# Turning attention's weights by way of DRAM and VectorE instead of TensorE

## The chip, the cores and the metric

The kernel runs on one core of a Trainium2 chip. A core has a matrix engine (TensorE, PE in the profile; its weight loads are PEld), VectorE (DVE), ScalarE (ACT), GpSimd (POOL) and SyncE (SP), an on-chip memory of 128 partitions, a matmul result memory (PSUM) of 8 banks of 128 x 512 f32, and 16 DMA engines to DRAM. The metric is the time of one execution in device microseconds. All data are f32.

## The reference

The input is two images of 128 channels by 64 x 64 pixels. Layer 0 is a group norm, a neighbourhood attention of 7 x 7 and two small feed-forward steps. Layer 1 takes each image as 4096 tokens of 128 numbers. Its attention is plain, with q for queries, keys and values alike, and each token barred from itself:

```python
def _L1_attn_ref(q):                      # q: (2, 4096, 128), layer-normed tokens
    scale = 1.0 / np.sqrt(128)
    sim = jnp.einsum('blh,bmh->blm', q, q) * scale
    sim = jnp.where(jnp.eye(4096, dtype=bool)[None], -1e9, sim)
    attn = jax.nn.softmax(sim, axis=-1)
    return jnp.einsum('blm,bmh->blh', attn, q)

t = t + _L1_attn_ref(_ln_t(t))
t = t + _L1_ffn_ref(_ln_t(t), sigma, phi, M_u, M_phi_plus, M_phi_minus, log_weights, gumbel)
```

The second part (`_L1_ffn_ref`) is a long convolution with 16 filters, summed through 32 matrices of 128 x 128, with three short lags, in one of four branches that the weights pick. The diff does not touch what is computed.

## The kernel before

The program has three stages. Layer 0 runs first (to about 345 us), in an order written out by hand. Then layer 1's attention runs for image 0 and image 1 (345 to 1256 us). Last comes the convolution (to the end), written by hand for TensorE. The attention stage stands outside such a hand-made order: the framework places the instructions on the engines' queues, and in the trace TensorE's order within a pair is that of the source. On its queue an engine runs its instructions in order.

**Attention by pairs of chunks.** The 4096 tokens are 8 chunks of 512. Because q serves as query and key, the scores are symmetric, and each pair (a, c) of chunks with a <= c is computed once: 36 pairs an image, 8 of them on the diagonal. For a pair, the helper `weights(a, c, k)` is called for k = 0 to 3. Each call makes one score product of 128 tokens of chunk a by 512 tokens of chunk c (line 918, into a PSUM tile `bank`), and ScalarE takes the exponential into a tile `e` and sums its rows into `part` (line 926). The scores of the next pair are made while the present pair's are used.

A weight block has two uses. As it lies, with chunk a's tokens on the partitions, it is the right operand of the products that add to chunk c's output (PSUM tile `other`, line 983). For chunk a's output it must be turned, so that chunk c's tokens lie on the partitions. `turned(a, c, m, es)` does that: four TensorE transposes of 128 x 128 into a `bank` (line 942), and one VectorE operation that copies them to the tile `et` and sums the rows (line 945). Then `onto` multiplies `et` and adds to chunk a's output (PSUM tile `own`, line 956). These products wait in the list `late` and follow within two steps. A pair off the diagonal thus has 4 score products, 4 `other` products, 16 transposes and 4 `own` products. At the end of a pair VectorE adds `other` to the result `xa` (lines 995 and 997), and when a chunk's last product is in, it adds `own` (lines 960 and 962). `other` and `own` have one PSUM buffer each, `bank` has six.

On the diagonal, only the upper blocks are computed; `weights` turns the earlier ones by TensorE (line 932), and one VectorE operation copies and sums them (line 933). Line 924 adds a large negative number to the diagonal of the scores.

**Fill work.** After each of a pair's four steps `fill()` takes one piece from a list of other work: what is left of layer 0 (`drain`), the filters' transforms (`filters`, GpSimd's additions at line 1246), the tokens of image 1 (`tokens`), the layer norm and transform of each finished chunk (`after`, lines 1010 to 1071, with GpSimd's power at line 173 between VectorE's operations), the short lags (`short_lags`, line 1101), and the mixing of 32 matrices from loaded tiles `st` (`mixed`, lines 1171 to 1176). The transformed tokens are stored to DRAM by SP (`us`, lines 1043 and 1048).

GpSimd issues four DMAs in all (line 795, loads of image 1 at the start). ScalarE's queue issues a few near the start (lines 300 to 304). All other DMAs are on SP's queue.

Of the kernel before, what the change touches and what calls it, by code (L numbers as in the profile page):

```python
# [8 lines left out]
F32 = mybir.dt.float32  # L9
# [14 lines left out]
MASKED = -1.0e30  # L24

# [76 lines left out]
def kernel(  # L102
# [767 lines left out]
    with ap_:  # L870
        tp = ap_.enter_context(tc.tile_pool(name="l1_t", bufs=1, side="right"))
        ep = ap_.enter_context(tc.tile_pool(name="l1_e", bufs=8, side="right"))
        sp = ap_.enter_context(tc.tile_pool(name="l1_s", bufs=2, side="right"))
        ps_o = ap_.enter_context(tc.tile_pool(name="l1_ps_o", bufs=1, space=PSUM))
        ps_m = ap_.enter_context(tc.tile_pool(name="l1_ps_m", bufs=6, space=PSUM))
# [13 lines left out]
        one = tp.tile([P, 512], F32, name="one")  # L889
        nc.gpsimd.memset(one, 1.0)  # L890
# [6 lines left out]
        def attention(b, fill):  # L897
# [12 lines left out]
            pairs = [(a, c) for a in range(8) for c in range(a, 8)]  # L910
            chunk = lambda a: slice(CHUNKS[a] * 512, (CHUNKS[a] + 1) * 512)

            def weights(a, c, k, left=()):
# [3 lines left out]
                ps = bank()  # L917
                nc.tensor.matmul(  # L918
                    ps[:, lo:], lhsT=cm[b][:, n * P : (n + 1) * P],
                    rhs=cm[b][:, CHUNKS[c] * 512 + lo : (CHUNKS[c] + 1) * 512], start=True, stop=True,  # L920
# [4 lines left out]
                e = ep.tile([P, 512], F32, tag="e", name="e")  # L925
# [3 lines left out]
                if lo:  # L929
                    pt = bank()  # L930
                    for j in range(k):
                        nc.tensor.transpose(pt[:, j * P : (j + 1) * P], left[j][:, lo : lo + P], ident)
                    nc.vector.tensor_tensor_reduce(
                        e[:, 0:lo], pt[:, 0:lo], one[:, 0:lo], 1.0, 0.0, ALU.mult, ALU.add, part[:, n, 8:9]
                    )
                return e

            def turned(a, c, m, es):

                pt = bank()  # L940
                for k in range(4):
                    nc.tensor.transpose(pt[:, k * P : (k + 1) * P], es[k][:, m * P : (m + 1) * P], ident)  # L942
                et = ep.tile([P, 512], F32, tag="et", name="et", bufs=4)
                n = 4 * CHUNKS[c] + m
                nc.vector.tensor_tensor_reduce(  # L945
                    et, pt, one, 1.0, 0.0, ALU.mult, ALU.add, part[:, n, a : a + 1]
                )
                return et

            own = None  # L950

            def onto(a, n, e, first, last):
                nonlocal own
                if first:
                    own = ps_o.tile([P, 512], F32, tag="own", name="own")
                nc.tensor.matmul(own, lhsT=tok[b][:, n, :], rhs=e, start=first, stop=last)  # L956
                if last:
                    xs = xa[b][:, chunk(a)]
                    if a:
# [762 lines left out]
```

## Time and profile before

| What | Value |
|---|---|
| Median of 3 runs | 2070.3 us (2065.34 to 2070.57) |
| The profiled execution: its own time | 2070.71 us |
| The profiled execution: span from first to last instruction | 2068.7 us |
| Mean granted TensorE clock | 0.989 |
| `turned`'s transposes, line 942 | 896, of 273 ns (median) each, overlapping |
| Their evictions, line 945 | 224, of 686 ns (median) each |
| `own` products from `et`, line 956 | 448 passes, two a product |
| `other` products, line 983 | 448 passes, two a product |
| Largest group of the run, line 1436 (convolution) | 206.2 us of VectorE |

The profile is of one execution. It gives every instruction its engine, source line, start and duration. "Idle before" is the time that an engine stood still before a group of instructions, with the instruction that ended the wait. Matmuls overlap: a row's mean duration is longer than the distance between two of them, so the cost of one in a row is read from the distance of the starts. Every f32 product of 512 columns is recorded as two passes. "GB/s" and "DMA share" are what the 16 DMA engines moved and how busy they were. The chain is the line of work that ended last, followed back from the end.

### The profile page before, as it was taken

The page shows a single profiled execution, that of the slowest core. Times are in us where ns is not written, and L with a number is a line of the kernel's source. Part 1 is how long each engine was busy: PE and PEld are TensorE (multiplying, and loading weights), DVE is VectorE, ACT ScalarE, POOL GpSimd, SP SyncE. Part 2 cuts the span into 40 slices and gives each one's busy share as a digit, 9 for nine tenths or more (in the row PEclk, how much of TensorE's full clock was granted, in tenths as well). Part 3 has the DMA queues.
Part 4 walks back from the last instruction along what each step waited for, and adds up shares of the span by engine and source line. Part 5 has one row for each costly group of instructions (what it writes and reads, how often), then busy time and mean ns, then how long its engine had stood idle before and what let it go on. Part 6 is the DMA issues. An engine that isn't in the chain of part 4 may idle for free.

```text
span 2068.7 us, 52809 instructions
## 1 busy us (share of the span) xinstructions
PE 1997.5 (97%) x21368; PEld 1436.1 (69%) x21368; DVE 997.7 (48%) x3458; ACT 733.5 (35%) x1974; POOL 472.9 (23%) x781
## 2 busy tenths in 40 slices
PE   6899998999999999999999999999999999999998
PEld 4677775554555554554455554799999899999987
DVE  5899996444544445335733446333333333333332
ACT  3789885322322323212222322222222222222222
POOL 4466887215000000000000000022222121222211
PEclk8999999999999999999999999999999999999999
DMA  4222223003000001004200002222222123222211
GB/s 152 62 61 62 61 60 53 13 21 107 2 25 26 26 26 52 26 0 117 83 26 26 26 26 77 76 67 67 67 67 61 47 58 101 66 67 67 67 45 42
DMA packets 239506, 112.82 MB, mean 55 GB/s; under 512 B 118287, under 2 KB 237215, under 8 KB 238752
## 3 DMA queue, kind: packets, MB, share of 16 engines
q1 hardware_dynamic: 238338, 105.95, 18.9%
q8 instruction: 169, 2.77, 0.6%
q0 software_dynamic: 576, 2.10, 0.3%
q10 hardware_dynamic: 350, 1.41, 0.2%
q14 instruction: 73, 0.60, 0.1%
HBM read 74.78 MB, written 34.63 MB: 53 GB/s over the span
## 4 chain that ended last, share of the span: by engine, by line
PE 80%; DVE 7%; DMA 4%; POOL 4%; ACT 2%; SPq 2%; issue 1%; DVEq 0%; POOLq 0%; ACTq 0%
PE acc L1450 27%; PE own L956 11%; PE bank L918 9%; PE other L983 8%; PE pc L1431 7%; PE bank L942 4%; PE bank L343 2%; PE bank L201 1%; PE bank L1058 1%; PE bank L553 1%; DMA st<-in_m_minus_dram 1%; DMA st<-in_m_plus_dram 1%; ACT p L540 1%; PE bank L1101 1%; PE pc L1489 1%
## 5 line engine op out<-in xcount | busy, mean ns | idle before, releaser
L1436 DVE COPY y<-pc 128x512 f32<-128x512 f32 x320 | 206.2, 686 | 351.4 <-PE pc L1431 351.2
L926 ACT ACTIVATE e<-bank 128x512 f32<-128x512 f32 (+3 forms) x288 | 161.6, 561 | 519.6 <-PE bank L918 396.5
L1450 PE MATMUL acc<-y,mpl 32*128 32x256 f32 x5120 | 324.4, 380 | 0.8 <-DVE af L1460 0.8
L1450 PE MATMUL acc<-y,mmi 32*128 32x256 f32 x5120 | 316.7, 375 | 0.0
L1436 ACT COPY y<-pc 128x512 f32<-128x512 f32 x320 | 171.9, 589 | 400.9 <-PE pc L1431 396.1
L1450 PEld LDWEIGHTS acc<-y,mpl 32*128 32x128 f32 x5120 | 290.0, 186 | 8.2 <-DVE af L1460 1.8
L1450 PEld LDWEIGHTS acc<-y,mmi 32*128 32x128 f32 x5120 | 291.4, 185 | 3.8
L918 PE MATMUL bank<-cm 128*128 128x512 f32 (+3 forms) x576 | 277.4, 564 | 1.4 <-DVE y L664 1.4
L956 PE MATMUL own<-et,tok 128*128 128x512 f32 x448 | 230.2, 600 | 8.4 <-DVE part L945 8.1
L983 PE MATMUL other<-e,tok 128*128 128x512 f32 x448 | 229.9, 595 | 4.9 <-DVE xa L995 4.9
L1431 PE MATMUL pc<-ct,ut 32*128 32x256 f32 x2560 | 215.6, 382 | 5.6 <-DMA ut<-us 3.7
L945 DVE CUSTOM_DVE_ANT_0 et<-bank,one 128x512 f32<-128x512 f32 x224 | 146.1, 687 | 128.6 <-PE bank L942 128.4
L1461 POOL TENSOR_TENSOR af<-af 128x512 f32<-128x512 f32 x39 | 49.7, 1275 | 593.8 <-DVE af L1460 528.1
L173 POOL TENSOR_TENSOR ln_rs<-ln_rs,mhalf 128x4 f32<-128x4 f32 x24 | 24.2, 1009 | 703.6 <-DVE ln_rs L172 703.5
L1431 PEld LDWEIGHTS pc<-ct,ut 32*128 32x128 f32 x2560 | 175.7, 189 | 12.0 <-DMA ut<-us 4.5
L956 PEld LDWEIGHTS own<-et,tok 128*128 128x128 f32 x448 | 82.9, 190 | 121.8 <-issue 60.8
L983 PEld LDWEIGHTS other<-e,tok 128*128 128x128 f32 x448 | 81.7, 190 | 95.0 <-issue 86.9
L942 PEld LDWEIGHTS bank<-ident,e 128*128 128x128 f32 x896 | 103.0, 141 | 46.1 <-issue 39.4
L918 PEld LDWEIGHTS bank<-cm 128*128 128x128 f32 x576 | 94.5, 191 | 54.2 <-issue 38.9
L540 ACT ACTIVATE p<-p,mn 128x196 f32<-128x196 f32 x256 | 114.4, 449 | 13.7 <-DVE mn L530 13.0
L942 PE MATMUL bank<-ident,e 128*128 128x128 f32 x896 | 117.1, 274 | 0.0
L1039 DVE TENSOR_TENSOR ub<-bank,uo 128x256 f32<-128x256 f32 (+1 forms) x192 | 59.5, 373 | 71.1 <-ACT uo L1036 70.2
(258 smaller groups left out, 2530.8 us busy)
## 6 DMA issues: line engine op xcount, KB each, us to landing
ut<-us SPq DMA_DIRECT2D x160, 128.0 KB
us<-ub SPq DMA_DIRECT2D x128, 128.0 KB
ct<-gs SPq DMA_DIRECT2D x320, 40.0 KB
vw<-vd SPq DMA_DIRECT2D x256, 49.0 KB
ct<-gs SPq DMA_DIRECT2D x320, 32.0 KB
vd<-v SPq DMA_DIRECT2D x128, 32.0 KB
st<-in_m_plus_dram SPq DMA_DIRECT2D x16, 256.0 KB
us<-ub SPq DMA_DIRECT2D x128, 32.0 KB
```

The costliest lines, as they stand in the source:

```text
L540: nc.scalar.activation(p, p, AF.Exp, bias=t[name + "mn"][:, h : h + 1], scale=-1.0, accum_out=t["den"][:, u, h : h + 1],)
L918: nc.tensor.matmul(ps[:, lo:], lhsT=cm[b][:, n * P : (n + 1) * P], rhs=cm[b][:, CHUNKS[c] * 512 + lo : (CHUNKS[c] + 1) * 512], start=True, ...
L926: nc.scalar.activation(e[:, lo:], ps[:, lo:], AF.Exp, bias=0.0, scale=ASCALE, accum_out=part[:, n, c : c + 1])
L942: nc.tensor.transpose(pt[:, k * P : (k + 1) * P], es[k][:, m * P : (m + 1) * P], ident)
L945: nc.vector.tensor_tensor_reduce(et, pt, one, 1.0, 0.0, ALU.mult, ALU.add, part[:, n, a : a + 1])
L956: nc.tensor.matmul(own, lhsT=tok[b][:, n, :], rhs=e, start=first, stop=last)
L983: nc.tensor.matmul(other, lhsT=tok[b][:, 4 * CHUNKS[a] + j, :], rhs=es[j], start=(j == 0), stop=(j == 3))
L1039: nc.vector.tensor_tensor(ub[:, sgn, 0:n], pu[s][:, 0:n], half[:, 0:n], op)
L1431: nc.tensor.matmul(pcs[j].rearrange("p (g o c) -> p o g c", g=4, o=2)[:, :, at], lhsT=ut[rows_, par, :], rhs=cv_[rows_], start=True, stop= ...
L1436: (nc.scalar.copy if j % 2 else nc.vector.tensor_copy)(y[:, :, :, 4 * kl + j, :], pcs[j].rearrange("p (g x k) -> p k g x", g=4, k=KF))
L1450: nc.tensor.matmul(acc[j][:, 0:256], lhsT=(mmi if l else mpl)[rows_, k, :], rhs=y[rows_, k, 2 * l : 2 * l + 2].rearrange("p s n x -> p (s ...
L1461: eng.tensor_tensor(af[:, 0:2], af[:, 0:2], af[:, 2:4], ALU.add)
```

## The change

The 27 off-diagonal pairs of each image other than (6, 7) no longer use `turned`'s transposes on TensorE. Their weights take this way:

1. `weights` makes the scores with chunk c's tokens in another order (32-token groups q = 0 to 3 outermost, then the four 128-token tiles), and the four exponentials of a pair go to one tile `e` of 128 x 2048.
2. `sent`: when the fourth is done, ScalarE's queue writes that tile to a DRAM tile `eb` with one DMA of 1 MB.
3. `moved`: two steps later (`MOVE`) GpSimd issues four reads of 256 KB, one for each q. They put each 32-token group on its own 32 partitions of a tile `et`.
4. `turned`: five steps after sending (`TURN`) VectorE turns 32 x 32 blocks in place, by two transposes of 128 x 1024, and sums rows over the 2048 elements of each partition into `part`, in one operation.
5. `pair_onto`: six steps after (`DELAY`) the four `own` products follow, up to two a step, from strided views of `et` into a strided view of `own`.

A step is one of a pair's four turns of the inner loop. `own` gets a second PSUM buffer and `bank` loses one (six to five). Pair (6, 7), next to last in the order, keeps TensorE's transposes (`turned_here`), with ScalarE to copy and sum. The diagonal's copy and sum become two VectorE operations. To make room, the filters' tiles `ph` and `sums` move into `cm[1]`, which is filled later.

```diff
-        ep = ap_.enter_context(tc.tile_pool(name="l1_e", bufs=8, side="right"))
+        ep = ap_.enter_context(tc.tile_pool(name="l1_e", bufs=2, side="right"))
-        ps_m = ap_.enter_context(tc.tile_pool(name="l1_ps_m", bufs=6, space=PSUM))
+        ps_m = ap_.enter_context(tc.tile_pool(name="l1_ps_m", bufs=5, space=PSUM))
...
+            far = lambda a, c: a != c and (a, c) != (6, 7)
...
+                if far(a, c):
+                    nc.tensor.matmul(
+                        ps.rearrange("p (q t j) -> p q t j", q=4, t=4), lhsT=cm[b][:, n * P : (n + 1) * P],
+                        rhs=keys.rearrange("p (t q j) -> p q t j", t=4, q=4), start=True, stop=True,
+                    )
+                    e = eh.rearrange("p (q k r) -> p k q r", q=4, k=4)[:, k]
+                    nc.scalar.activation(
+                        e, ps.rearrange("p (q r) -> p q r", q=4), AF.Exp, bias=0.0, scale=ASCALE,
+                        accum_out=part[:, n, c : c + 1],
+                    )
+                    return e
...
-                    nc.vector.tensor_tensor_reduce(
-                        e[:, 0:lo], pt[:, 0:lo], one[:, 0:lo], 1.0, 0.0, ALU.mult, ALU.add, part[:, n, 8:9]
+                    nc.vector.tensor_copy(e[:, 0:lo], pt[:, 0:lo])
+                    nc.vector.tensor_reduce(part[:, n, 8:9], e[:, 0:lo], AX.X, ALU.add)
...
+            def sent(eh):
+                eb = dram.tile([P, 4, 512], F32, tag="eb", name="eb", bufs=4)
+                nc.scalar.dma_start(out=eb.rearrange("p q r -> p (q r)"), in_=eh)
+                return eb
+
+            def moved(eb):
+                et = ep.tile([P, 4, 512], F32, tag="et", name="et", bufs=2)
+                for q in range(4):
+                    nc.gpsimd.dma_start(
+                        out=et[32 * q : 32 * q + 32], in_=eb[:, q].rearrange("(h p) r -> p h r", h=4)
                     )
+                return et
+
+            def turned(et, a, c):
+                for q in (0, 2):
+                    flat = et[:, q : q + 2].rearrange("p q r -> p (q r)")
+                    nc.vector.transpose(flat, flat)
+                n0 = 4 * CHUNKS[c]
+                nc.vector.tensor_reduce(
+                    part[:, n0 : n0 + 4, a], et.rearrange("p q (k t i) -> p t (q k) i", k=4, t=4), AX.XY, ALU.add
+                )
...
+            def pair_onto(own, a, c, et, t):
...
+                onto(
+                    own, 4 * CHUNKS[c] + t, own.rearrange("p (k q i) -> p q k i", k=4, q=4),
+                    et.rearrange("p q (k t i) -> p t q k i", k=4, t=4)[:, t], False, c == 7 and t == 3,
+                )
...
+            def pass_on(n):
+                while coming_ and coming_[0][0] + MOVE <= step:
+                    at, eb, a, c = coming_.pop(0)
+                    et = moved(eb)
+                    turns.append((at + TURN, et, a, c))
+                    late.extend((at + DELAY, a, c, et, t) for t in range(4))
+                while turns and turns[0][0] <= step:
+                    turned(*turns.pop(0)[1:])
+                while n and late and late[0][0] <= step:
+                    _, a, c, et, t = late.pop(0)
+                    pair_onto(owns[a], a, c, et, t)
+                    n -= 1
...
+                for j in range(4):
+                    if following:
+                        coming.append(coming_of(*following, j, coming, halves))
...
+                    pass_on(2)
+                    fill()
+                    step += 1
```

## The prediction

> **What bounds the kernel now.** I read the page's busy shares first, then the windows of the stage that the diff touches, then the timeline of one pair there, then the waits.
>
> ```profile
> PE 1997.5 (97%) x21368; PEld 1436.1 (69%) x21368; DVE 997.7 (48%) x3458; ACT 733.5 (35%) x1974; POOL 472.9 (23%) x781
> ...
> PE 80%; DVE 7%; DMA 4%; POOL 4%; ACT 2%; SPq 2%; issue 1%; DVEq 0%; POOLq 0%; ACTq 0%
> ...
> 350.00:802.00 452.00, 444.98 (x1732) 234.06 (x1731) 207.25 (x761) 129.24 (x366) 70.85 (x79) 1.00 0.13 33
> 802.00:1256.00 454.00, 444.14 (x1679) 227.88 (x1678) 212.60 (x687) 119.84 (x352) 7.55 (x8) 1.00 0.15 43
> ```
>
> The windows are the two batches of attention. TensorE is idle 17 of 906 us there, VectorE is busy 46%, ScalarE 27%, GpSimd 9%, the DMA engines 13 to 15%, and the granted clock is 1.00. So TensorE's work sets the stage's time; the chain (TensorE 80%) says the same. Work taken off TensorE shortens the run as long as nothing makes TensorE wait.
>
> ```profile
> 905.50 1.04 PE L942 MATMUL bank<-ident,e 128*128 128x128 f32 x8
> 906.38 1.02 PE L918 MATMUL bank<-cm 128*128 128x512 f32 x2
> 907.24 1.02 PE L983 MATMUL other<-e,tok 128*128 128x512 f32 x2
> 907.50 0.60 ACT L926 ACTIVATE e<-bank 128x512 f32<-128x512 f32 x1 [2.76 <-PE bank L918]
> 907.99 0.20 ACT L926 ACTIVATION_READ_ACCUMULATOR e<-bank 128x1 f32 x1
> 908.09 1.02 PE L956 MATMUL own<-et,tok 128*128 128x512 f32 x2
> 908.95 1.02 PE L918 MATMUL bank<-cm 128*128 128x512 f32 x2
> ...
> 911.53 1.04 PE L942 MATMUL bank<-ident,e 128*128 128x128 f32 x8
> ```
>
> Half a pair, from one set of eight transposes to the next, takes 6.03 us. From start to start eight transposes cost 0.88 us (905.50 to 906.38), so 0.110 us each, and one 512-column product (two passes) 0.86 us. Six products and the transposes make 6.02, so here there is no gap at all. A whole pair is 12.04 us, 1.76 of it transposes.
>
> **The change, part by part.** *Transposes removed.* 27 of the 28 off-diagonal pairs of each batch lose 16 transposes: 54 x 1.76 = 95.0 us off TensorE's path. A pair becomes 4 steps of 10.28 us in all. The evictions at line 945 go too, and with them the waits of TensorE for them (8.1 us idle before line 956 in the groups of the page).
>
> *Products through strided views.* The scores, `other` and `own` products keep their count but read runs of 32 or 128 elements, and `own` is written in runs of 32. The identity products at line 1611 read every second element at 388 to 400 ns, as line 1058 does with plain rows (401, 402); line 1431 writes PSUM in runs of 64 at 382 beside 375 to 380 at line 1450. I take 0. Were each of the 12 products 5% dearer, it would be 54 x 12 x 0.043 = 28 us.
>
> *The round trip.* Call T0 the start of a pair's fourth score product, one pair ahead of its use. The exponential and its sum end at T0 + 1.81 (906.38 to 908.19 above). Then ScalarE issues one write of 1 MB. The nearest row has the same shape, the two 1 MB stores at the kernel's end:
>
> ```profile
> 2061.31 2.09 SPq L1540 DMA_DIRECT2D out_dram<-o  x2
> ...
> 2062.00:2063.00 1.00, 0.00 (x0) 0.00 (x0) 0.99 (x3) 0.94 (x3) 0.00 (x0) 0.67 0.94 393
> 2064.00:2065.00 1.00, 0.00 (x0) 0.00 (x0) 0.00 (x0) 0.00 (x0) 0.00 (x0) 0.50 1.03 426
> 2067.00:2068.70 1.70, 0.00 (x0) 0.00 (x0) 0.00 (x0) 0.00 (x0) 0.00 (x0) 0.50 0.02 5
> ...
> 19.34 2.42 POOL L795 DMA_DIRECT2D xa<-in_x_dram  x4
> ...
> DMA to landing us min/median/max: 5.4/6.5/7.6
> ```
>
> Transfer starts some 0.8 us after the issue and 1 MB at about 400 GB/s is 2.6; the landing adds between 0 and 1.7 (the last row's tail). I take 3.9 us, bounds 3.4 and 5.1. GpSimd then waits for that write and issues four reads of 256 KB. Its four issues at line 795 took 2.42 us and their 512 KB landed 5.4 us or more after the issue. Below: last issue at 1.8 plus 2.7 (a 256 KB `st` load in the chain, 2.70 to 3.06), 4.5; above: 2.42 + 5.4 = 7.8, which is for twice the bytes. I take 5.3, nearer the load of equal size. With 0.2 for two semaphores the data are there at T0 + 1.8 + 3.9 + 5.3 + 0.2 = 11.2, bounds 9.9 and 14.9.
>
> *VectorE.* No row shows its transpose. Rows of 128, 256 and 512 f32 columns (0.29, 0.42, 0.69 us at lines 1466, 1462, 995) give 0.15 + 1.06 ns an element: 1.23 us for one of 1024. Bounds: twice the fastest 512-column row, 481 ns at line 1174, 0.96; and GpSimd's 1275 ns for 512 at line 1461 doubled, 2.55. The sum over 2048 elements is 2.31. VectorE goes from 4 x 0.77 + 0.69 = 3.77 to 5.46 us per pair (2.46 + 2.31 + 0.69), of 10.3: still not the bound, and its share in the stage rises from 46% to about 64%.
>
> *The wait that this adds for `own`.* Its products stand six steps after T0. The steps hold 2, 4, 4 and 2 products, so they are due at T0 + 15.4 (18 products of 0.86). VectorE's two transposes are queued behind the addition of `other` to `xa`, which can only begin when the pair's last `other` product has ended at T0 + 12.0. Addition 0.9 with its semaphore, transposes 2.46: T0 + 15.4. So VectorE's own queue, not the transfer (11.2 + 2.5 = 13.7), ends last, with no slack: I take 0.15 us a pair, 8 us. With transposes of 2.55 it is 2.6 us a pair, 140 us; if the scheduler puts them ahead of the addition, 0.
>
> *`other` has one PSUM buffer.* Its next first product must wait for that same addition. Before, an `own` product, eight transposes and a score product (2.6 us) covered it (4.9 us idle in all, line 983). Now only the score product's 0.86 is left against some 0.97: 0.11 us a pair where VectorE is free. I take 0.2, 11 us; one 0.69 us operation ahead of it each time would make 0.8, 43 us; 0 if fill work stands between.
>
> *GpSimd and SP.* GpSimd now holds 2.4 us of issues a pair and waits some microseconds for the write. Behind it queue the power of each layer norm (line 173, 1.01 us, for which VectorE waits) and the filters' additions (line 1246). SP's `st` loads and `us` stores share the DMA engines: 2 MB a pair at 400 GB/s are 5.2 of 10.3 us, so the busy share goes from 15% to about 65%. The two stretches that already wait for these:
>
> ```profile
> 475.00:500.00 25.00, 24.08 (x111) 11.63 (x110) 8.16 (x20) 5.81 (x17) 17.79 (x19) 1.00 0.39 125
> 945.00:1030.00 85.00, 76.49 (x250) 37.21 (x248) 56.55 (x157) 16.23 (x50) 1.01 (x1) 1.00 0.38 108
> ```
>
> In the second, VectorE waits for one `st` load after another and is 67% busy. Six pairs there may not gain their 1.76 us, and 32 loads may each be late: 13 us taken, between 0 and 50. The first: 6, between 0 and 25. One score bank fewer (5 for 6) while VectorE is held 4.8 us at a time: 5, between 0 and 20. The diagonal's copy and sum in place of one operation (48 times some 0.4 us) lies on VectorE outside its tight spot: 0. ScalarE's issue (0.6 us, as at line 304) lies in its 73% of idle time. The filters' tiles moved into `cm[1]`: 0.
>
> **Sum.** -95.0 - 8.1 + 8 + 11 + 13 + 6 + 5 = -60. The profiled execution took 2070.7 us, 2.0 beyond its span of 2068.7, and the median of the runs is 2070.3, so both bases agree. 2070.7 - 60 gives **2010 us**.
>
> **Two rules from the Trainium skill weighed.** "VectorE: DVE Perf Modes", section "The three transpose paths", gives 390 ns for TensorE and 311 for VectorE on 128x128 of two-byte data, and its rules prefer TensorE where PSUM may be the target. By its 390 the change would gain 54 x 16 x 0.39 = 337 us; the trace's spacing of 110 ns, in a row of eight, decides. "SBUF — State Buffer", section "Who interferes with whom", says that VectorE's two-port modes starve DMAs issued by GpSimd, with 620 ns growing to 3100; by that, four issues would be late by up to 10 us and the change would lose. No run here shows it; the four issues at 19.34 us ran at 0.61 each beside VectorE's work from PSUM.
>
> **Rivals.** *A: VectorE's queue is tighter (faster, but less).* Transposes of some 1.7 us, or an operation in front of the addition, give 0.5 to 1 us more per pair: 27 to 54 us, so 2037 to 2064. For it: no slack at T0 + 15.4. Against: the queue is nearly free at that moment.
>
> *B: slower, the transposed weights come too late.* Between T0 and its `own` products lie two such waits (the pair before's and its own), so lateness of the transfer costs half per pair; lateness on VectorE costs all. The 60 us are gone at 1.1 us more per pair: data 2.2 us behind the 12.9 that is just in time (T0 + 15.1), or transposes of 1.8 us each. At its upper bound of 14.9 the transfer alone costs 54 x 1.0 us and leaves 2064; the transposes at theirs, 2.55, cost 140 - 8 = 132 and give 2142. For it: the DMA engines at 65% and `st` loads beside. Against: 1 MB at 400 GB/s is seen twice.
>
> *C: the scheduler puts transposes ahead of the addition, and fill work covers `other`:* none of the 43 us of new waits but the stretches' 13: 1980.
>
> **How the numbers follow.** The likeliest case 0.54 (1988 to 2032, with half and one and a half times the 43 us of new waits), A 0.15, B 0.22, C 0.06, and 0.03 for a gain and waits that cancel within 0.3% (6 us, about what a measurement of this kernel can tell from no change). Faster 0.75, same 0.03, slower 0.22. The range 1972 to 2095 leaves out most of B's upper half and some of C.
>
> **What would show it.** Line 942's transposes fall from 896 to 32. TensorE's busy time in attention falls by some 95 us. Right: idle before `own` and `other` under 0.5 us a pair, its releaser VectorE; the write landing within 4 us and the reads within 6. Wrong: VectorE waiting for the reads by microseconds, a transpose of 2 us or more, strided products above 600 ns, or attention's DMA share near 1.

## The result: slower by 2.3%, and the profile after

The changed kernel takes 2115.1 us (median of 4 runs, 2112.9 to 2119.7) against 2068.4 for the kernel before on the same chip, a ratio of 1.023 (95% interval 1.0205 to 1.0254). The forecast was 2010 us, with 2095 as the top of its range. The profiled execution took 2113.3 us, span 2111.6, mean granted clock 0.969 (before: 0.989).

First the page of the changed kernel: busy time, DMA queues (packets, MB, share of 16 engines), and the groups that the forecast priced.

```profile
PE 1942.4 (92%) x20504; PEld 1356.1 (64%) x20504; DVE 1112.5 (53%) x3172; ACT 735.7 (35%) x1990; POOL 592.0 (28%) x996
...
q0 software_dynamic: 17856, 58.73, 12.3%
q10 hardware_dynamic: 8126, 58.04, 6.9%
...
L1052 PE MATMUL other<-e,tok 128*128 128x512 f32 x448 | 232.4, 621 | 30.0 <-DVE xa L1069 13.3
L987 PE MATMUL own<-et,tok 128*128 128x512 f32 x448 | 213.7, 616 | 36.3 <-DVE et L970 36.1
...
L970 DVE STREAM_TRANSPOSE et<-et 128x1024 f32<-128x1024 f32 x108 | 128.0, 1220 | 27.3 <-DMA et<-eb 27.2
...
L972 DVE TENSOR_REDUCE part<-et 128x4 f32<-128x2048 f32 x54 | 123.2, 2282 | 1.1
...
et<-eb POOLq DMA_DIRECT2D x216, 256.0 KB, 5.6
```

A transpose on VectorE takes 1.22 us and the sum 2.28, as forecast, and 864 transposes are gone from TensorE. Each read lands 5.6 us after its own issue (median). What differs most is idle time. These are the stage as a whole, then the two stretches that the forecast had named, and the one behind them (columns: stretch, length, busy time of PE, PEld, DVE, ACT, POOL, then granted clock, DMA share, GB/s). The kernel before:

```profile
345.00:1295.00 950.00, 925.73 (x3568) 480.62 (x3568) 449.47 (x1568) 258.23 (x740) 85.33 (x95) 1.00 0.14 40
1030.00:1100.00 70.00, 69.91 (x258) 36.12 (x258) 27.23 (x89) 18.35 (x55) 1.01 (x1) 1.00 0.07 19
```

The changed kernel:

```profile
345.00:1341.00 996.00, 873.59 (x2714) 401.58 (x2712) 566.36 (x1286) 259.99 (x758) 206.28 (x312) 0.96 0.54 152
475.00:500.00 25.00, 17.76 (x77) 7.58 (x76) 9.19 (x29) 7.36 (x20) 13.89 (x18) 0.95 0.72 230
945.00:1030.00 85.00, 67.71 (x173) 29.32 (x174) 44.28 (x92) 20.25 (x62) 12.64 (x22) 0.88 0.73 205
1030.00:1100.00 70.00, 45.07 (x116) 18.81 (x115) 44.23 (x85) 11.70 (x33) 7.59 (x13) 0.80 0.60 164
```

In the stage TensorE was idle for 24 of 950 us; now it is idle for 122 of 996. Its busy time fell by 52 us, not by 95. The granted clock in the stage fell from 1.00 to 0.96, and to 0.80 in the last stretch; by estimate, the 831 us of work that are left (926 less 95) would take 865 at 0.96, which is most of the difference. The convolution's first product (line 1431 before, 1511 after) starts at 1341.1 instead of 1295.7 us; nothing is lost behind that.

What ended VectorE's idle time, in DMAs alone (columns: us in total, times, longest). The kernel before:

```profile
DVE mpl L1176 <- DMA st<-in_m_plus_dram: 12.5, 6, 4.5
DVE mmi L1176 <- DMA st<-in_m_minus_dram: 8.9, 11, 1.6
DVE ph L1208 <- DMA pn<-in_phi_pad_dram: 4.5, 3, 2.0
...
DVE ub L1039 <- DMA us<-ub: 0.6, 1, 0.6
```

The changed kernel:

```profile
DVE ub L1118 <- DMA us<-ub: 45.7, 16, 7.0
DVE et L970 <- DMA et<-eb: 27.2, 10, 4.5
DVE mpl L1255 <- DMA st<-in_m_plus_dram: 15.7, 3, 10.1
DVE mmi L1255 <- DMA st<-in_m_minus_dram: 15.4, 4, 7.4
DVE cm L1288 <- DMA pn<-in_phi_pad_dram: 10.6, 2, 9.6
```

VectorE waits for SyncE's transfers (`us`, `st`, `pn`, `gs`) for 97 us instead of 30, and for the new reads for 27. The chain through the stage agrees: its pieces that are DMAs sum to 185 us instead of 67, those for `us` stores to 76 instead of 10. One wait for `st`, seen on two engines: VectorE's row of instructions in the stretch of the `st` loads, and TensorE's idle time at that place.

```profile
1042.33 0.48 DVE L1253 TENSOR_SCALAR mmi<-st,wt 128x512 f32<-128x512 f32 x1 [2.16 <-DMA st<-in_m_minus_dram]
1047.97 0.75 DVE L1255 SCALAR_TENSOR_TENSOR mmi<-st,wt,mmi 128x512 f32<-128x512 f32 x1 [5.16 <-DMA st<-in_m_minus_dram]
1048.64 1.24 DVE L970 STREAM_TRANSPOSE et<-et 128x1024 f32<-128x1024 f32 x1
1050.50 0.75 DVE L1255 SCALAR_TENSOR_TENSOR mmi<-st,wt,mmi 128x512 f32<-128x512 f32 x1 [0.62 <-DMA st<-in_m_minus_dram]
1051.17 1.24 DVE L970 STREAM_TRANSPOSE et<-et 128x1024 f32<-128x1024 f32 x1
```
```profile
1035.93 3.70 PE L987 MATMUL own<-et,tok 128*128 128x512 f32 x8 [1.68 <-DVE et L970]
1052.46 3.78 PE L987 MATMUL own<-et,tok 128*128 128x512 f32 x4 [12.83 <-DVE et L970]
```

A mixing operation waits 5.16 us for its `st` load and the next one 0.62 us for its own; a pair's two transposes stand behind them on VectorE's queue; TensorE stands still for 12.83 us. In the chain the second load is a piece of 7.57 us. The chain before has fifteen such pieces in the stretch of these loads, twelve of 2.70 to 3.06 us and the longest of 4.42. TensorE is also slower afterwards: four passes take 3.78 us where eight took 3.70, and the granted clock is 0.52 from 1043 to 1057 us.

### The profile page after: what moved, and what is told of

Same layout as the page of the kernel before. It is cut to its first block, busy times and chain, and to the rows that moved or that the text cites. A ratio compares the mean times of both kernels' runs of the same rounds, so it can differ in the third digit from the quotient of the medians.

```text
span 2111.6 us, 51431 instructions
## 1 busy us (share of the span) xinstructions
PE 1942.4 (92%) x20504; PEld 1356.1 (64%) x20504; DVE 1112.5 (53%) x3172; ACT 735.7 (35%) x1990; POOL 592.0 (28%) x996
## 3 DMA queue, kind: packets, MB, share of 16 engines
q1 hardware_dynamic: 238338, 105.95, 18.7%
q0 software_dynamic: 17856, 58.73, 12.3%
## 4 chain that ended last, share of the span: by engine, by line
PE 57%; DMA 9%; DVE 7%; POOL 2%; issue 2%; SPq 1%; ACT 1%; DVEq 0%; POOLq 0%; ACTq 0%
PE acc L1530 27%; PE own L987 8%; PE pc L1511 7%; PE other L1052 5%; PE bank L923 4%; DMA us<-ub 4%; DMA et<-eb 2%; PE bank L933 2%; DVE et L970 1%; DMA st<-in_m_minus_dram 1%; PE bank L202 1%; DMA st<-in_m_plus_dram 1%; PE bank L1180 1%; PE pc L1569 1%; POOL ln_rs L174 1%
## 5 line engine op out<-in xcount | busy, mean ns | idle before, releaser
L928 ACT ACTIVATE e<-bank 128x512 f32<-128x512 f32 x216 | 129.3, 599 | 411.9 <-PE bank L923 395.2
L987 PE MATMUL own<-et,tok 128*128 128x512 f32 x448 | 213.7, 616 | 36.3 <-DVE et L970 36.1
L961 POOL DMA_DIRECT2D et<-eb x216 | 119.3, 558 | 415.4 <-DMA eb<-e 143.1
L923 PE MATMUL bank<-cm 128*128 128x512 f32 x432 | 222.8, 612 | 9.2 <-DVE ub L1118 8.9
L970 DVE STREAM_TRANSPOSE et<-et 128x1024 f32<-128x1024 f32 x108 | 128.0, 1220 | 27.3 <-DMA et<-eb 27.2
L923 PEld LDWEIGHTS bank<-cm 128*128 128x128 f32 x432 | 76.7, 195 | 84.3 <-issue 69.5
L972 DVE TENSOR_REDUCE part<-et 128x4 f32<-128x2048 f32 x54 | 123.2, 2282 | 1.1
L541 ACT ACTIVATE p<-p,mn 128x196 f32<-128x196 f32 x256 | 114.4, 449 | 12.9 <-DVE mn L531 12.3
```

Of the source, the lines that this page charges most:

```text
L541: nc.scalar.activation(p, p, AF.Exp, bias=t[name + "mn"][:, h : h + 1], scale=-1.0, accum_out=t["den"][:, u, h : h + 1],)
L923: nc.tensor.matmul(ps.rearrange("p (q t j) -> p q t j", q=4, t=4), lhsT=cm[b][:, n * P : (n + 1) * P], rhs=keys.rearrange("p (t q j) -> p ...
L928: nc.scalar.activation(e, ps.rearrange("p (q r) -> p q r", q=4), AF.Exp, bias=0.0, scale=ASCALE, accum_out=part[:, n, c : c + 1],)
L961: nc.gpsimd.dma_start(out=et[32 * q : 32 * q + 32], in_=eb[:, q].rearrange("(h p) r -> p h r", h=4))
L970: nc.vector.transpose(flat, flat)
L972: nc.vector.tensor_reduce(part[:, n0 : n0 + 4, a], et.rearrange("p q (k t i) -> p t (q k) i", k=4, t=4), AX.XY, ALU.add)
```

## The experiments

Each ratio is to the kernel before on the same chip, with its 95% interval. Differences between runs are of medians; by the ratios they come out up to 3 us apart. Lines of a diff that only repeat others are left out. T0 is the forecast's: the start of a pair's fourth score product. The framework places the instructions of every kernel anew, so the runs differ in their order too; where this bears on a reading it is said. Two theories. *Theory 1:* the transfers delay SyncE's loads and stores, VectorE waits for them in order, and TensorE behind VectorE. *Theory 2:* waits and queues of the new way itself: VectorE's order, GpSimd held by its waits, one PSUM bank fewer, two `et` buffers.

### Do the transfers cost it? e1 and e6

```diff
-nc.scalar.dma_start(out=eb.rearrange("p q r -> p (q r)"), in_=eh)
+nc.scalar.dma_start(out=eb[:, :, 0:32], in_=eh.rearrange("p (q r) -> p q r", q=4)[:, :, 0:32])
-out=et[32 * q : 32 * q + 32], in_=eb[:, q].rearrange("(h p) r -> p h r", h=4)
+out=et[32 * q : 32 * q + 32, :, 0:32], in_=eb[:, q, 0:32].rearrange("(h p) r -> p h r", h=4)
```

> The changed kernel with every write and read cut to one sixteenth: 32 of the 512 elements of each run are moved (64 KB instead of 1 MB per write and per set of four reads), into two buffers that are kept and filled once; the rest of the turned weights is stale, so the output is not the reference's. Number of transfers, queues, waits, VectorE's transposes and sums, TensorE's products: all as in the changed kernel. Theory 1 (the transfers themselves: large packets beside SyncE's small ones make us stores, st and pn loads late, VectorE waits for those in order, TensorE's gaps then cost clock): most of the 105 us between forecast and result come back, 2010 to 2045 us. Theory 2 (waits and queues: VectorE's order, one PSUM bank fewer, GpSimd held by its waits, two et buffers): 2090 to 2115 us, us and st landings short all the same.

Measured: 2020.2 us (2019.7 to 2022.7), ratio 0.9767 (0.9752 to 0.9782). Every queue, buffer and instruction of the change is there, and the kernel is 50 us faster than before, close to the forecast's 60. But one wait is not there, although the expectation says so: the 32 columns that the small write takes all come from the first of the pair's four exponentials. One pair of e1 (first exponential, write, fourth score product, transposes):

```profile
418.10 0.60 ACT L937 ACTIVATE e<-bank 128x512 f32<-128x512 f32 x1 [2.78 <-PE bank L932]
418.81 0.52 ACTq L963 DMA_DIRECT2D eb<-e  x1
426.51 1.02 PE L932 MATMUL bank<-cm 128*128 128x512 f32 x2
427.00 2.37 DVE L979 STREAM_TRANSPOSE et<-et 128x1024 f32<-128x1024 f32 x2 [1.32 <-DMA et<-eb]
```

Over the 54 pairs e1's write leaves 8.0 us before T0 and the transposes start at T0 + 0.4 (medians); in the changed kernel the write leaves at T0 + 1.8. So the 95 us between e1 and the changed kernel are for the bytes and for this wait together. e6 puts the write back (the first pair of lines above undone), and with it the wait for all four exponentials:

> e1 with the full write of 1 MB per pair and the reads still at one sixteenth; the output is not the reference's for the same reason as in e1. It divides the 95 us between e1 and the changed kernel. Bytes alike: 2060 to 2075. The write's 8-KB packets: 2085 to 2110. The reads: 2020 to 2040.

Measured: 2022.6 us (2019.4 to 2025.0), ratio 0.9771 (0.9753 to 0.9789). The whole write, 1 MB per pair in packets of 8 KB, costs 2 us together with its wait. Theory 2 would have left 2090 us or more, so it falls. The reads of the same 1 MB, added to the write, cost 93 more. No run has the full reads beside a small write, so it is not shown whether reads are dear as such or the second megabyte is. The 93 us also hold another order of instructions: VectorE's queue has the same instruction in 82% of its places in both kernels, TensorE's in 94%. VectorE's waits in e6:

```profile
DVE et L979 <- DMA et<-eb: 85.6, 30, 11.4
DVE mpl L1264 <- DMA st<-in_m_plus_dram: 7.9, 3, 6.5
DVE cm L1297 <- DMA pn<-in_phi_pad_dram: 6.2, 2, 4.2
DVE mmi L1264 <- DMA st<-in_m_minus_dram: 5.2, 5, 1.8
```

Those for SyncE's transfers are 25 us in all and none is for `us` (in the chain `us` stores sum to 6 us). It waits three times as long for `et` as in the changed kernel, in a kernel that is 93 us faster. Two other ways in which the bytes could cost time are not seen: the engines' own instructions are as fast in both (medians: a transpose 1.23 us, an exponential 0.60), and VectorE waits less for GpSimd, whose work stands behind the reads, in the changed kernel (41 us) than in e6 (63) or before (54).

### The same transfers beside the kernel before: e2 and e5

e2 adds, to the kernel before, a write that hangs on nothing:

```diff
+nc.scalar.dma_start(out=eb.rearrange("p q r -> p (q r)"), in_=tok[b][:, 0:16, :].rearrange("p n c -> p (n c)"))
 ...
+for q in range(4):
+    nc.gpsimd.dma_start(out=idle_to[32 * q : 32 * q + 32], in_=eb[:, q, 0:448].rearrange("(h p) r -> p h r", h=4))
```

> The kernel before with its TensorE transposes, and beside it the change's transfers with their data unused: per far pair one write of 1 MB by ScalarE's queue (from the normalized tokens) two steps later four reads by GpSimd's queue (448 of 512 columns, 7/8 of the bytes, for want of room); ph and the filter sums lie in cm[1] as in the changed kernel. Theory 1: 40 to 120 us slower than before, 2110 to 2190, lost in the stretches with us stores, filters and st loads (us landing from 1.9 to 5 us and more). Theory 2: at most 15 us slower, 2070 to 2085.

Measured: 2110.4 us (2108.9 to 2111.3), ratio 1.020 (1.0185 to 1.0215). The size fits Theory 1, but the run is not what it was meant to be. What the instructions that touch `idle_to` and `eb` show (count, duration, first and last start):

```profile
L981 POOL DMA_DIRECT2D idle_to<-eb x216: 550/550/679, 352.4 to 917.1; - x108
L972 ACTq DMA_DIRECT2D eb<-tok x54: 326/326/1216, 310.9 to 682.8; - x54
```

All writes had left by 683 us and all reads by 917, before the `st` stretch. e5 ties them to the exponentials:

```diff
-nc.scalar.dma_start(out=eb.rearrange("p q r -> p (q r)"), in_=tok[b][:, 0:16, :].rearrange("p n c -> p (n c)"))
+for q in range(4):
+    nc.scalar.dma_start(out=eb[:, q], in_=es_[q])
```

> The kernel before with the same idle transfers as e2, now tied to the work: the write of a pair is four transfers of 256 KB, one from each of its four e tiles, so they cannot leave before the exponentials; four reads by GpSimd's queue follow (7/8 of the bytes, data unused). In e2 the writes hung on nothing and ran ahead: all transfers lay before 920 us, and after 850 us the kernel lost nothing. Theory 1 (transfers delay SyncE's loads and stores, whatever VectorE does): lost in both batches, 2100 to 2165 us. Rival 1b (they cost much only where VectorE carries the 5 us of transposes and sums per pair as well): batch 1 loses under 10 us, 2070 to 2095.

Measured: 2101.3 us (2099.0 to 2103.5), ratio 1.0154 (1.0134 to 1.0174): 31 us for the write and the reads together, although no engine computes with these data; GpSimd waits for the writes, and ScalarE 8 us for tiles that they still read. The order is that of the kernel before in 99% of TensorE's places and 95% of VectorE's. VectorE's waits for SyncE's transfers rise from 30 to 50 us. Batch 1 loses about half of the 31, more than rival 1b allows. This table shows where: how much later than in the kernel before a pair's first score product starts.

| image, pair | before, us | changed | e5 | e6 | e12 |
|---|---|---|---|---|---|
| 0, (1, 2) | 454.6 | +2.0 | +6.1 | -2.7 | -8.2 |
| 0, (2, 2) | 542.0 | +10.9 | +15.1 | -4.6 | -8.5 |
| 0, (6, 6) | 759.1 | +7.5 | +15.7 | -15.7 | -27.9 |
| 1, (1, 2) | 923.8 | +4.8 | +15.6 | -21.7 | -30.9 |
| 1, (2, 5) | 1042.4 | +44.5 | +32.3 | -26.4 | -35.4 |
| 1, (6, 6) | 1220.8 | +36.8 | +32.1 | -43.8 | -50.3 |

e5 loses in two stretches alone: filters and first stores up to (2, 2) of image 0, and the `st` loads of image 1. Between them it loses nothing. The changed kernel loses more in the second (+40 there) and fails to gain in between: the 14 changed pairs from (2, 2) to (6, 6) of image 0 win it 3 us, while e6 wins 11 and e12 19.

### Which property of the reads: e3, e4, e10

e3 writes in pieces of 2 KB:

```diff
-eb = dram.tile([P, 4, 512], F32, tag="eb", name="eb", bufs=4)
+eb = dram.tile([P, 4, 640], F32, tag="eb", name="eb", bufs=4)[:, :, 0:512]
```

> The changed kernel with the DRAM rows padded, so that the write leaves in pieces of 2 KB instead of 8 KB (the reads already go in runs of 2 KB). Same bytes. If the DMA engines take turns between queues packet by packet, SyncE's 512-byte packets wait a quarter as long during a write: us stores land in about 4 us instead of 6 to 7, 2085 to 2105 us. If only the bytes count, or the reads are what holds them: 2110 to 2120 us as the changed kernel.

Measured: 2100.8 us (2096.1 to 2102.0), ratio 1.015 (1.0128 to 1.0171): 14 us better. VectorE's longest wait for `us` falls from 7.0 to 5.1 us, but its waits for SyncE's transfers sum to 115 us, not less than 97. The order of instructions is the changed kernel's (VectorE's in every place). So the write's long pieces cost 14 us beside the full reads, inside the first expectation, and by which wait is not shown; beside e6's small reads the same pieces cost next to nothing.

The Trainium skill, "DMA: Bandwidth & Descriptors", section "Queues, rings and completion order", says that each DMA engine takes turns between its queues packet by packet. By that rule a long packet of either direction would hold SyncE's short ones up. e3 fits it; e6 and the 93 us of the reads do not fit it alone, and no run here shows the turns themselves.

e4 has the reads on another queue:

```diff
-nc.gpsimd.dma_start(
+nc.sync.dma_start(
```

> The changed kernel with the four reads of a pair issued by SyncE's queue instead of GpSimd's. In the changed kernel's trace GpSimd's queue moves its bytes at about half the rate per packet of the others, and GpSimd waits for the write and for a free et buffer with layer norm's power behind it. If GpSimd's queue (slow reads, power late) is what costs: 2050 to 2085 us. If it is the bytes beside SyncE's small transfers: 2095 to 2130, since us stores and st loads now also stand in order behind reads that wait.

Measured: 2114.7 us (2112.0 to 2119.4), ratio 1.0224 (1.0205 to 1.0243), the changed kernel's time. But the waits change places. VectorE's for `us` are gone, since the stores now stand in order with the reads, and those for the reads nearly triple:

```profile
DVE et L970 <- DMA et<-eb: 72.9, 16, 10.5
```

TensorE also waits 72.9 us for VectorE's `et` here, against 36.1. VectorE's waits for SyncE's transfers are 26 us, as in e6, and the time is lost all the same: here the trace shows the loss as late weights (first transpose at T0 + 29.3, median). The forecast had weighed the rule of the Trainium skill, "SBUF — State Buffer", section "Who interferes with whom", that VectorE's two-port modes starve DMAs issued by GpSimd. In the changed kernel GpSimd's issues take 550 ns (median), 679 at most, and off its queue the time is the same; no run here shows that this costs anything.

e10 moves the exchange of blocks to the write, so that the read is one transfer of 8 KB per partition:

```diff
-nc.scalar.dma_start(out=eb.rearrange("p q r -> p (q r)"), in_=eh)
+for h in range(4):
+    nc.scalar.dma_start(out=eb[:, :, h].rearrange("q p r -> p q r"),
+                        in_=eh[32 * h : 32 * h + 32].rearrange("p (q r) -> p q r", q=4))
...
+nc.gpsimd.dma_start(out=et.rearrange("p h r -> p (h r)"), in_=eb.rearrange("q p h r -> (q p) (h r)"))
```

> The changed kernel with the exchange of blocks moved from the reads to the write: four writes of 256 KB by ScalarE's queue (32 partitions each, in runs of 2 KB) into DRAM ordered as et, and one read of 1 MB by GpSimd's queue, 8 KB in a row per partition. Same bytes, GpSimd issues 0.6 us instead of 2.2 us per pair. In the changed kernel a read packet of 4 KB takes about 285 ns and a write packet of 8 KB 320. If the reads cost through the time that their short runs hold the engines: 2040 to 2085. If through their bytes: 2100 to 2125.

Measured: 2182.9 us (2178.3 to 2186.9), ratio 1.0532 (1.0507 to 1.0558), a miss on both sides. Queues and waits:

```profile
q10 hardware_dynamic: 31454, 58.05, 10.3%
q0 software_dynamic: 8352, 58.72, 8.2%
```
```profile
ACT e L928 <- DMA eb<-e: 55.7, 10, 15.3
```

The reads' share fell from 12.3 to 8.2%, but the write's rose from 6.9 to 10.3%. ScalarE waits for `e` buffers that slow writes hold, a wait that the changed kernel does not have. That a shorter read would help is thus neither shown nor refuted.

### Where: e8

```diff
-far = lambda a, c: a != c and (a, c) != (6, 7)
+here_ = ((0, 5), (2, 0)) if b == 0 else ((1, 4), (2, 6))
+far = lambda a, c: a != c and (a, c) != (6, 7) and not here_[0] <= (a, c) < here_[1]
```

> The changed kernel with TensorE's transposes kept (as the last pair's) in the pairs beside which SyncE is busiest: batch 0 (0,5) to (1,7), filters and first us stores, and batch 1 (1,4) to (2,5), the st loads. Sixteen pairs give up 1.76 us each, 28 us. Theory 1 with the loss in these stretches (lag grew by 18 and by 38 us there): 2070 to 2090. Loss spread evenly over all pairs: 2110 to 2140.

Measured: 2057.5 us (2054.9 to 2063.7), ratio 0.9945 (0.9923 to 0.9967). Sixteen pairs give up 28 us, and the kernel becomes 58 us faster than the changed one, and faster than before. By estimate these 16 of the 54 pairs had then cost 58 + 28 = 86 us, more than Theory 1 had expected of the two stretches.

### Fewer bytes, one trip: e7, e12, e11, e15

The exchange of blocks needs no DRAM: sixteen copies of 64 KB per pair go straight from `e` to `et`.

```diff
-eb = dram.tile([P, 4, 512], F32, tag="eb", name="eb", bufs=4)
-nc.scalar.dma_start(out=eb.rearrange("p q r -> p (q r)"), in_=eh)
-return eb
+return eh
...
-    nc.gpsimd.dma_start(
-        out=et[32 * q : 32 * q + 32], in_=eb[:, q].rearrange("(h p) r -> p h r", h=4)
-    )
+    for h in range(4):
+        (nc.gpsimd if h % 2 else nc.sync).dma_start(
+            out=et[32 * q : 32 * q + 32, h], in_=eb[32 * h : 32 * h + 32, 512 * q : 512 * q + 512]
+        )
```

> The changed kernel without DRAM: sixteen copies of 64 KB per pair (32 partitions of 2 KB) straight from e to et, eight by SyncE's queue and eight by GpSimd's; the rest unchanged. Half of the bytes that the DMA engines carry, no wait for a write. Theory 1: about half of the 95 us return, 2050 to 2080 us. If it is the wait at the queues and the number of issues that count (GpSimd 4.4 us of issues per pair, SyncE eight more): 2100 to 2150.

Measured: 2033.1 us (2028.6 to 2036.3), ratio 0.9821 (0.9801 to 0.9841): 82 of the 95 us come back, in a kernel that leaves nothing out, with half of the change's bytes. e12 takes the step's pause away that the write had needed (`MOVE, TURN, DELAY = 1, 5, 6`):

> e7 with MOVE 1 instead of 2: the copies are issued a step, 2.6 us, earlier, since nothing is written first; queues as in e7. If lateness of the copies is left of e7's loss: 2022 to 2032. If they wait for an et buffer all the same: 2031 to 2040.

Measured: 2018.0 us (2013.8 to 2020.7), ratio **0.9735 (0.9716 to 0.9755)**: as fast as e1, which moved hardly any bytes, and 55 us faster than before. The queues, VectorE's waits and the stage of e12:

```profile
q1 hardware_dynamic: 259074, 134.29, 24.6%
q0 software_dynamic: 14400, 30.44, 5.8%
```
```profile
DVE et L969 <- DMA et<-e: 67.8, 22, 11.9
DVE mmi L1254 <- DMA st<-in_m_minus_dram: 9.5, 10, 1.9
DVE mpl L1254 <- DMA st<-in_m_plus_dram: 5.6, 3, 4.7
...
DVE ub L1117 <- DMA us<-ub: 1.3, 2, 1.1
```
```profile
345.00:1250.00 905.00, 854.95 (x2749) 398.67 (x2748) 561.54 (x1288) 265.72 (x760) 300.78 (x527) 0.98 0.39 105
```

Waits for SyncE's transfers are back at 23 us, TensorE is idle for 50 us in the stage, and the clock is 0.98. VectorE waits 68 us for `et`, more than in the changed kernel, and this is the fastest of the kernels. The queue shares give the engines' time for a pair: (12.3 + 6.9)% of 2111.6 us is 405, less the 10 that these queues took before (0.5%), over 54 pairs 7.3 us; here 5.8% + 0.3% + (24.6 - 19.6)% of 2012 is 223, less 10, 4.0 us (19.6% is what SyncE's other transfers take, 18.7% of 2111.6 us).

e11 issues half of the copies from ScalarE's queue (`nc.scalar` in the place of `nc.sync`):

> e7 with eight of a pair's sixteen copies on ScalarE's queue instead of SyncE's (0.33 us each, 2.6 us of ScalarE per pair), and one step earlier (MOVE 1). In e7 VectorE waited 80 us for et and ScalarE 58 us for e held by copies that stood behind us stores on SyncE's queue. If that queue is what is left of e7's loss against e1: 2015 to 2030. If ScalarE, waiting for an et buffer, delays its exponentials: 2035 to 2070.

Measured: 2045.5 us (2043.5 to 2048.0), ratio 0.9867 (0.9848 to 0.9886), 28 us worse than e12. The rival's case: ScalarE, whose exponentials every pair needs, stands for copies, for 100 us where it is 24 in e12.

```profile
ACT e L928 <- DMA et<-e: 99.5, 25, 8.9
```

e15 takes e12 with `MOVE, TURN, DELAY = 1, 4, 5`:

> e12 with the transposes and the own products a step earlier (TURN 4, DELAY 5): the copies land some 2 us after they are issued, so the data are there, and et buffers and e buffers come free 2.6 us sooner. If waits for these buffers are left in e12: 2005 to 2015. If nothing is left there: 2014 to 2022.

Measured: 2027.6 us (2026.2 to 2031.6), ratio 0.9794 (0.9775 to 0.9812), worse by 10 us and outside both expectations. VectorE then waits 101 us for `et` instead of 68.

### Lateness or delay: e9, e14, e13, e16

Do the reads' bytes cost by making the turned weights late (rival B) or by delaying SyncE's transfers? e9 only asks the source for later reads, in e1 (`MOVE, TURN, DELAY = 5, 5, 6`):

> e1 (one sixteenth of the bytes, output not the reference's) with MOVE 5 instead of 2: the reads are issued three steps, some 7.7 us, later, so that the turned weights arrive about 15 us after T0, as late as in the changed kernel, without its bytes. Rival B of the forecast (lateness costs half per pair; break-even at T0 + 15.1): 2060 to 2080 us. Theory 1 (the reads cost by delaying SyncE's transfers, for which VectorE stands): 2018 to 2035.

Measured: 2020.8 us (2014.1 to 2023.1), ratio 0.9745 (0.9724 to 0.9767). It tells nothing: the framework put the reads where they had been, 3.7 us after the write's issue (median), in e1 3.6. e14 makes them wait for a transfer that cannot come earlier:

```diff
+if behind_:
+    nc.scalar.dma_start(out=behind_.pop()[:, 0, 31:32], in_=halves[0][:, 2047:2048])
```

> e1 (one sixteenth of the bytes, output not the reference's) with the reads of a pair made to wait for 512 bytes that ScalarE's queue writes into the same block after the last exponential of the pair that follows: 10.3 us later, so that the small reads land at about T0 + 16, as in the changed kernel. Rival B: half of 1 us or more per pair against its break-even of T0 + 15.1, 2045 to 2080. Theory 1: 2015 to 2040.

Measured: 2043.8 us (2040.1 to 2047.1), ratio 0.9868 (0.9849 to 0.9887). GpSimd now waits in every pair:

```profile
POOL et L970 <- DMA eb<-e: 299.5, 54, 13.1
```

How late a pair's data are, counted from T0 (medians of 54 pairs):

| run | data landed | first transpose | time, us |
|---|---|---|---|
| e1 | -0.1 | 0.4 | 2020.2 |
| e6 | 10.8 | 11.8 | 2022.6 |
| e13 | 14.0 | 16.1 | 2098.7 |
| e14 | 14.9 | 19.5 | 2043.8 |
| changed | 18.9 | 23.2 | 2115.1 |

So e14 has half of the lateness that the changed kernel has against e6 (by the landing; two thirds by the transposes), not all of it as its expectation says. It costs 24 us against e1 and 21 against e6, just above Theory 1's range and below rival B's. What the full lateness costs no run shows. e13 gives the bytes back without the need for them, behind e6's small reads:

```diff
+idle = dram.tile([P, 4, 512], F32, tag="idle", name="idle", bufs=4)
+for q in range(4):
+    nc.gpsimd.dma_start(out=idle[32 * q : 32 * q + 32], in_=eb[:, q].rearrange("(h p) r -> p h r", h=4))
```

> e6 (full write, reads of one sixteenth that VectorE uses, output not the reference's) plus, behind the small reads of a pair, four copies of 256 KB by GpSimd's queue from the written block to another place in DRAM, in runs of 2 KB as the full reads have, their data unused. The reads' bytes are back, nobody waits for them. Delay of SyncE's transfers (theory 1): 2070 to 2115 us. Lateness (rival B): 2025 to 2055.

Measured: 2098.7 us (2094.8 to 2105.8), ratio 1.0128 (1.0103 to 1.0152): 76 us more than e6 for bytes that nobody waits for. VectorE's waits:

```profile
DVE et L984 <- DMA et<-eb: 69.2, 23, 10.7
DVE mpl L1269 <- DMA st<-in_m_plus_dram: 20.6, 7, 12.2
DVE ub L1132 <- DMA us<-ub: 15.9, 12, 3.4
DVE mmi L1269 <- DMA st<-in_m_minus_dram: 14.6, 8, 4.7
```

Those for `et` are below e6's; those for SyncE's transfers rise from 25 to 64 us. Yet the small reads stood behind the copies on one queue (first transpose at T0 + 16.1, in e6 11.8), so some of the 76 is lateness. It is less late than e14, whose lateness costs 21 us more than e6: by estimate at least 55 of the 76 are something else. e16 put the copies on ScalarE's queue, from the block of the pair before:

> e13 with the idle copies on ScalarE's queue, right behind a pair's write, and from the block of the pair before, which has long landed: GpSimd's queue holds only the small reads, as in e6 (output not the reference's for the same reason). If the 76 us of e13 are delay of SyncE's transfers and of the stages that wait for them: 2065 to 2100 us, with VectorE's waits for st, us and pn well above e6's 25 us and those for et at e6's 85. If they were lateness of the small reads behind the copies: 2025 to 2050.

Measured: 2251.8 us (2250.2 to 2254.3), ratio 1.0876 (1.0857 to 1.0895), far outside both. It does not separate them: the next pair's write now stood behind the copies, and GpSimd waited 323 us for written blocks. It shows what a jam in the trip's own queue costs.

What stands: the reads' bytes, added to the write's, cost 93 us, in the order that the framework gives each kernel. Lateness of the turned weights is not the whole: bytes that nobody waits for cost 31 us beside the kernel before (write and reads) and 76 beside e6, some 55 of them not lateness. In the changed kernel and in e13 the traces show these bytes as waits for SyncE's transfers (97 and 64 us instead of e6's 25) with the transposes behind them; in e4 they show as waits for `et`. So the delay of SyncE's transfers is seen, but that it is the larger part of the 93 is argued. The split, the share of the order, and why the reads cost so much and the write so little stay open.

## Why the prediction was wrong

**Removed transposes, right.** TensorE has 864 instructions fewer. Its busy time falls by 81 us in e12 (1997.5 to 1916.8), where the clock in the stage is 0.98; in the changed kernel by 55.

**Strided products, right.** From the start of one pass to the next it is 429 ns (median) for score, `own` and `other` products, in the kernel before, the changed one and e12 alike.

**Round trip, mis-sized: the second step that failed.** The forecast had the data at T0 + 11.2, with bounds 9.9 and 14.9. In the changed kernel they land at T0 + 18.9 (median), at the earliest at T0 + 14.1, and in 41 of 54 pairs beyond the upper bound. The write's last packet ends 5.1 us after its issue (median, 3.5 to 9.4; 3.9 taken, at most 5.1). From the first read's issue to the last landing it is 8.1 us (median; 5.3 taken, at most 7.8). This is so even in a quiet pair: the write's issue is at 581.45 us, the reads' first at 585.88, the last landing at 593.98. The reads' price went by loads of the kernel before. VectorE then turns the data at T0 + 23.2, where the forecast's just in time is 12.9. The reads also waited for one of two `et` buffers, which the forecast had not counted:

```profile
POOL et L961 <- DMA eb<-e: 143.1, 15, 21.3
POOL et L961 <- PE own L987: 92.3, 8, 22.1
```

**VectorE's prices, right:** 1.22 us against 1.23, 2.28 against 2.31.

**The waits for `own` and `other`, near right without the bytes.** The forecast had 8 and 11 us more, less the 8.1 that it took off: 8.3 and 15.9 in all. In e12 the groups show 5.4 and 24.1 us of idle time, before 8.4 and 4.9. In the changed kernel they show 36.3 and 30.0: these rows carry the loss, but they are where it ends, not where it begins. e6, whose data land at T0 + 10.8, about where the forecast put them, takes 2022.6 us, 13 above the forecast.

**The step that failed** is "GpSimd and SP": "Six pairs there may not gain their 1.76 us, and 32 loads may each be late: 13 us taken, between 0 and 50. The first: 6, between 0 and 25." The DMA share was near (65% forecast, 0.54 in the stage, 0.73 in the stretch). Its price was not. In this term's place the reads' bytes, added to the write's, cost 93 us; the write and seven eighths of the reads cost 31 already beside the kernel before. Even both upper bounds give only 75. With it failed the round trip's T0 + 11.2, which has no term for the pair's own load on the DMA engines; by e14 lateness up to T0 + 14.9 costs 21 to 24 us, and what 18.9 costs is open. Three things were missed. VectorE runs in order, so a late `st` load delays the transposes queued behind it, and TensorE with them (12.83 us at 1052 us, behind two loads, one of 7.57 us). The `us` stores suffer all through the stage, not in two stretches: 46 us of VectorE's waits instead of 0.6. And the forecast had no term for the clock, which fell to 0.80 where TensorE idled.

**Rivals.** A (VectorE's transposes dearer) did not occur. B (the turned weights come too late) was on the right side, and its condition came true: data at T0 + 18.9, past its break-even of T0 + 15.1 and its upper bound of 14.9. Its price did not hold: half of what is beyond T0 + 12.9 would be 54 us for e14, where 21 to 24 were measured, 162 for the changed kernel, and 30 for e13, where 76 were. So B names a real part of the loss, not the whole. C (faster still) did not occur. No rival said that the new transfers would delay the old ones, though the forecast had the rows for it: small transfers on SyncE's queue for which VectorE already waited 30 us.

## What to carry to other kernels

When a change adds DMA traffic, price it by the transfers that are already there: find every wait for a DMA in the profile, ask what stands behind the waiting instruction, and do not take these waits as they were: here they grew from 30 to 97 us. Cutting a suspected transfer to a sixteenth tells its cost from that of the new way in one run, if what is left of it still waits for all that the whole waited for: e6's reads do, e1's write does not. Count lateness in such runs from the same event in each. Idle transfers beside the old kernel tell it from the other side, if a dependence ties them to their time. A block exchange between partitions can go from SBUF to SBUF in one trip, issued from queues whose engines hold up little: here that turned 2.3% slower into 2.6% faster.

## What the runs showed of the hardware

- 1 MB per pair written to DRAM cost 2 us in all beside small reads (e6 against e1); reading it back on top of that cost 93 more (changed kernel against e6, in another order of instructions).
- Sixteen SBUF-to-SBUF copies of 64 KB occupied the DMA engines for 4.0 us per pair, the DRAM round trip of the same 1 MB for 7.3; GpSimd's copies landed 2.7 us after issue (median).
- A write from 32 partitions at a time took more of the engines than one from 128 with the same 2-KB pieces: 10.3% in e10, and in e3, by its page, 7.5%. The layout in DRAM differs too.
- The granted clock was 0.80 in the stretch where TensorE was busy for 45 of 70 us, and 1.00 there before. Within it the clock was 0.52 from 1043 to 1057 us, around the wait of 12.83 us, and 1.00 in the 7 us before.
- In the stage SyncE's packets of 512 bytes took 27 ns each (median) before and in the changed kernel: these packets come late, they are not slower.
